# A fast matrix product for two of three channels, with its four PSUM banks in one tile

## The chip, the core and the metric

The kernel runs on one core of one Trainium2 chip. The metric is device time in microseconds, the median of several runs of one execution each. Lower is better. The engines are TensorE (PE, with its weight loads PEld), VectorE (DVE), ScalarE (ACT) and GpSimd (POOL); SyncE (SP) issues most DMAs.

## What is computed

A map x of 384 x 384 positions with 128 channels goes through two layers. Only the first one's middle matters here:

```python
z = layernorm(x)
left  = (z @ Wl + bl) * sigmoid(z @ Wlg + blg)
right = (z @ Wr + br) * sigmoid(z @ Wrg + brg)
core  = einsum('bikh,bjkh->bijh', left, right)      # 128 products of 384 x 384 x 384
zo    = layernorm(core) @ Wout + bout               # normalised over h
x1    = x + sigmoid(x @ Wg + bg) * zo
```

The second layer is a gated row update of x1. The norm over h after the core needs, for every position (i, j), the sum over channels of core and of its square.

## The kernel before

Three stages follow each other. Stage 1 makes left and right for all positions and writes them to DRAM (lr_d). Stage 2 forms the core, one channel h at a time. Stage 3 does the rest, row by row. The change touches stage 2 alone.

**Layout of stage 2.** N is 384, P is 128, NB is 3, J is N/2 = 192. A channel's left and right matrices lie in SBUF as three row blocks of 128 (index k of the product) by 384. `load_h(h)` loads both, interleaved, into `loaded2[h]` by two DMAs on SP's queue; three channels are in flight, and a channel's load is issued when TensorE has finished the channel three before. The last two groups of 64 positions never left SBUF (`kept`), and `stay(h)` copies them in on POOL. `apart(h, k)` (L632) copies block k of right out of the interleaved tile to `right[h]` on ScalarE.

**Two forms of the product.** For even h, `plain` issues nine products of 128 x 128 by 128 x 384 into `pc`, a PSUM tile of three banks, one bank for each row block of the result. For odd h a form after Strassen and Winograd covers the upper 256 rows: `left_sums` (four sums of 128 x 128 on POOL, L618) and `right_sums2` (three instructions on POOL, L623 to L628) form sums of blocks ahead of time, and TensorE then needs eleven half-width products (128 x 192) into `b0` to `b3`, besides three full ones into `b4` for the last 128 rows. In full widths this is 8.5 instead of 9. `b0` to `b4` are five PSUM tiles of one bank each. The order in the odd channel is:

1. the first product into b0; three into b4; ScalarE copies b0 to SBUF (`one`);
2. one product each into b1, b2, b3;
3. four adds on VectorE of 192 columns combine these (`base`, `more2`, `least`; L651);
4. seven more half products into b0, b1, b3, b2, the first of them into b0 again;
5. four more adds of 192 columns write the result's upper rows to SBUF (`ct`).

**Sums and stores.** ScalarE copies `pc` or `b4` to `ct`, squares each finished `ct` into `sq` (part of the SBUF tile `arena`, L635), and VectorE adds `ct` to `csum` (L638) and `sq` to `csq` (L642), 1152 columns at a time. For an even channel the sum is read from `pc`. `store_core` (L645) issues the DMA of `ct` to DRAM.

**What sets the order.** Every instruction passes through `seq`, which keeps each engine's instructions in the order of the text. The engines run side by side. The waits between them are placed by the tile framework from the tiles that each instruction reads and writes; the kernel states none. The last two channels (126 and 127) are written out after the loop and use `plain`'s order. All products of the loop pass through the helper `product` (L648), so that the profile tells them apart by their tiles: `pc` for the plain form, `b` for the other.

In stage 1, which isn't changed, one more PSUM tile of several banks matters for the prediction: `pr`, `[P, 2, 512]`. Two products (L372) fill its two banks; ScalarE reads both (L383), then VectorE (L385).

Of the kernel before, what the change touches and what calls it, by code (L numbers as in the profile page):

```python
# [8 lines left out]
F32 = mybir.dt.float32  # L9
# [5 lines left out]
P = 128  # L15
# [4 lines left out]
def triangle_then_gated_row_kernel(ctx: ExitStack, tc: tile.TileContext, a: dict, out: bass.AP):  # L20
# [35 lines left out]
    def seq(ins):  # L56

        return tc.keep_in_program_order(ins)
# [21 lines left out]
    with ExitStack() as ctx2:  # L80
# [480 lines left out]

        with tc.tile_pool(name="p2r", bufs=2, side="right", reuse_waits="tile") as rrp, \
             tc.tile_pool(name="p2more", bufs=1, side="right", reuse_waits="tile") as more, \
             tc.tile_pool(name="p2out", bufs=3, side="right", reuse_waits="tile") as op, \
             tc.tile_pool(name="p2st", bufs=1, side="right", reuse_waits="tile") as stp:
            csum = spool.tile([P, NB, N], F32, name="csum")
            csq = spool.tile([P, NB, N], F32, name="csq")
            seq(nc.vector.memset(csum, 0.0))
# [26 lines left out]

            J = N // 2
            js = slice(0, J), slice(J, N)
            one, base, more2, least = (arena[:, n, j] for n in (2, 2 * NB) for j in js)
            tt = arena[:, 0:2].rearrange("p b n -> p (b n)").rearrange("p (q j) -> p q j", j=J)
            ss = [arena[:, 2 * NB + 1, n * P:(n + 1) * P] for n in range(3)] + [stp.tile([P, P], F32, name="s4")]  # L600
            sq = arena[:, NB:2 * NB]
            cts = {}

            def block(h, k, i):
                return loaded2[h][:, k, i * P:(i + 1) * P, 0]

            def stay(h):

                for (kb, ig), lrt in kept.items():
                    seq(nc.gpsimd.tensor_copy(loaded2[h][:, kb, ig * G:(ig + 1) * G], lrt[:, h]))  # L610

            def left_sums(h):

                for n, x, y, op in ((0, block(h, 0, 1), block(h, 0, 0), ALU.subtract),
                                    (1, block(h, 0, 1), block(h, 1, 1), ALU.add),
                                    (2, ss[1], block(h, 0, 0), ALU.subtract),
                                    (3, block(h, 1, 0), ss[2], ALU.subtract)):
                    seq(nc.gpsimd.tensor_tensor(ss[n], x, y, op))  # L618

            def right_sums2(h):  # L620

                rr = right[h]
                seq(nc.gpsimd.tensor_tensor(  # L623
                    tt[:, 0:2], rr[:, 0, js[1]].unsqueeze(1).to_broadcast([P, 2, J]),
                    rr.rearrange("p b n -> p (b n)").rearrange("p (a m) -> p a m", a=2)[:, :, js[0]], ALU.subtract,
                ))
                seq(nc.gpsimd.tensor_tensor(tt[:, 2], rr[:, 0, js[0]], tt[:, 1], ALU.subtract))
                seq(nc.gpsimd.tensor_tensor(tt[:, 3], rr[:, 1, js[0]], tt[:, 2], ALU.subtract))  # L628

            def apart(h, k):  # L630

                seq(nc.scalar.copy(right[h][:, k], loaded2[h][:, k, :, 1]))  # L632

            def squares(h):
                seq(nc.scalar.activation(sq, cts[h], AF.Square))  # L635

            def add_sum(h, c=None):
                seq(nc.vector.tensor_add(csum, c or cts[h], csum))  # L638

            def add_squares(h):  # L640
                if h >= 0:
                    seq(nc.vector.tensor_add(csq, csq, sq))  # L642

            def store_core(h, queue=nc.sync):
                seq(queue.dma_start(out=core_d[:, h, :].rearrange("(b p) j -> p b j", p=P), in_=cts[h]))  # L645

            def product(to, lhsT, rhs, start=True, stop=True):
                seq(nc.tensor.matmul(to, lhsT=lhsT, rhs=rhs, start=start, stop=stop))  # L648

            def add(out, ps, term):  # L650
                seq(nc.vector.tensor_add(out, ps, term))  # L651

            def plain(h, banks):

                for k in range(NB):
                    for i in range(NB):
                        product(banks[i], block(h, k, i), right[h][:, k], k == 0, k == NB - 1)

            fill(0)
            with tc.tile_pool(name="p2mix", bufs=1, space=PSUM, reuse_waits="tile") as mps:  # L660
                pc = mps.tile([P, NB, 512], F32, name="pc")
                b0, b1, b2, b3 = (mps.tile([P, 512], F32, name="b%d" % n)[:, :J] for n in range(4))
                b4 = mps.tile([P, 512], F32, name="b4")[:, :N]
                for h in range(H - 2):
                    cts[h] = op.tile([P, NB, N], F32, tag="ct", name="ct")
                    right[h + 1] = rrp.tile([P, NB, N], F32, tag="rr", name="rr")
                    if h % 2 == 0:
                        plain(h, [pc[:, i, :N] for i in range(NB)])
                        if h > 0:
                            store_core(h - 1)  # L670
                        add_squares(h - 2)
                        stay(h + 1)
                        left_sums(h + 1)
                        for k in range(NB - 1):
                            apart(h + 1, k)
                        right_sums2(h + 1)
                        if h > 0:
                            squares(h - 1)
                            add_sum(h - 1)
                        apart(h + 1, NB - 1)  # L680
                        if h > 0:
                            add_squares(h - 1)
                    else:
                        rr, ct = right[h], cts[h]
# [4 lines left out]
                        seq(nc.scalar.copy(cts[h - 1], pc[:, :, :N]))  # L689
                        store_core(h - 1)  # L690
                        add_sum(h - 1, pc[:, :, :N])
                        seq(nc.scalar.copy(one, b0))
                        stay(h + 1)
                        for k in range(NB - 1):
                            apart(h + 1, k)
                        seq(nc.scalar.copy(ct[:, 2], b4))
                        apart(h + 1, NB - 1)
                        squares(h - 1)
                        product(b1, ss[2], tt[:, 2])
                        product(b2, ss[0], tt[:, 1])  # L700
                        product(b3, ss[1], tt[:, 0])
                        add(base, b1, one)
                        add(more2, b2, base)
                        add(base, b3, base)
                        add(least, b2, base)
                        product(b0, block(h, 1, 0), B[1][0], True, False)
                        product(b0, block(h, 2, 0), B[2][0], False, True)
                        product(b1, ss[3], B[1][1], True, False)
                        product(b1, block(h, 2, 0), B[2][1], False, True)
                        product(b3, block(h, 1, 1), tt[:, 3], True, False)  # L710
                        product(b3, block(h, 2, 1), B[2][0], False, True)
                        product(b2, block(h, 2, 1), B[2][1])
                        add(ct[:, 0, js[0]], b0, one)
                        add(ct[:, 0, js[1]], b1, base)
                        add(ct[:, 1, js[0]], b3, more2)
                        add(ct[:, 1, js[1]], b2, least)
                    del right[h], loaded2[h]
                    load_h(h + 3)
                store_core(h)
            with tc.tile_pool(name="p2ps", bufs=2, space=PSUM, reuse_waits="tile") as ps, \  # L720
                 tc.tile_pool(name="p2one", bufs=1, space=PSUM, reuse_waits="tile") as ps1:
                for h in range(H - 2, H):
# [11 lines left out]
                            start=(kb == 0), stop=(kb == NB - 1),  # L734
                        ))
                    if h == H - 2:
                        add_squares(h - 2)
                        squares(h - 1)
                        add_sum(h - 1)
                        add_squares(h - 1)  # L740
# [365 lines left out]
```

## Time and profile before

| | |
|---|---|
| median of 3 runs | 3137.58 us (3137.32 to 3138.57) |
| the profiled execution | 3139.36 us, its span 3137.6 us |
| granted TensorE clock | 0.999 |
| busy: PE, PEld, DVE, ACT, POOL | 99%, 70%, 82%, 62%, 76% of the span |
| stage 2 (the loop) | about 1012 to 1726 us of the span |
| HBM | 253 GB/s over the span |

The span runs from the first instruction to the last of one profiled execution; its own time is given by the device for the same execution and is 1.8 us longer. Matmul ends are modelled, so that a busy TensorE is not one at its peak. A line such as `L651 DVE TENSOR_TENSOR arena<-b,arena 128x192` names the line of the kernel, the engine, the operation, what it writes and reads, and the shape; after the bar come the busy time in us and the mean of one in ns, then the idle time of the engine ahead of the group, and what ended it.

### The profile page before, as it was taken

Reading aid. Unit: us, or ns where it says so; the run is one execution under the profiler, and the core shown is the slowest. Engines: PE = TensorE matmul, PEld = TensorE weight load, DVE = VectorE, ACT = ScalarE, POOL = GpSimd, SP = SyncE. Lnnn points to the kernel's source line nnn. Section 1 sums busy time; section 2 is a strip of 40 time slices with the busy share of each in tenths; the row PEclk is TensorE's granted clock in tenths of the full one; section 3 lists DMA queues with packets and bytes.
Section 4 is the critical chain, followed back from the end, with each engine's and each line's share of the span. In section 5 each row is a group of like instructions: output and inputs, shape, how many; then the busy total and the mean of one; then the engine's idle time right before and its main releaser. Section 6 shows DMA issues by size and latency. Waiting matters only on the chain.

```text
span 3137.6 us, 47186 instructions
## 1 busy us (share of the span) xinstructions
PE 3117.4 (99%) x11936; PEld 2209.1 (70%) x11936; DVE 2581.1 (82%) x7913; ACT 1949.7 (62%) x4196; POOL 2369.4 (76%) x3003
## 2 busy tenths in 40 slices
PE   9999999999999999999999999999999999999998
PEld 4677777777777777777777666777777777777776
DVE  8888888888886777777776888888888888888998
ACT  4444444444444666656666577777777777777776
POOL 6888888888886565666566588787887887888887
PEclk9999999999999999999999999999999999999999
DMA  4888978788883999999999866666666666666562
GB/s 153 327 312 293 334 276 332 287 321 311 292 333 89 288 289 291 291 290 290 290 290 290 296 213 221 217 222 222 222 222 222 220 223 215 222 218 222 205 216 105
DMA packets 509119, 797.61 MB, mean 254 GB/s; under 512 B 56689, under 2 KB 419569, under 8 KB 492466
## 3 DMA queue, kind: packets, MB, share of 16 engines
q1 hardware_dynamic: 507952, 793.20, 74.5%
q8 instruction: 100, 1.64, 0.2%
q14 instruction: 169, 1.38, 0.1%
q10 hardware_dynamic: 834, 1.18, 0.1%
q0 software_dynamic: 64, 0.20, 0.0%
HBM read 508.14 MB, written 286.36 MB: 253 GB/s over the span
## 4 chain that ended last, share of the span: by engine, by line
PE 98%; DVE 1%; ACT 0%; POOL 0%; issue 0%; DMA 0%; SPq 0%; POOLq 0%; DVEq 0%; ACTq 0%
PE pr L372 31%; PE pc L648 12%; PE b L648 11%; PE py L904 8%; PE pr L875 8%; PE pg L892 8%; PE pl L893 8%; PE pg L844 8%; PE py L905 4%; PE pc L732 0%; DMA stage<-in_x_nat_dram 0%; PE pq L852 0%; PE pt L335 0%; POOL rs L286 0%; DVE lr L385 0%
## 5 line engine op out<-in xcount | busy, mean ns | idle before, releaser
L372 PE MATMUL pr<-wz,xc 128*128 128x512 f32 x2176 | 935.2, 592 | 1.4 <-POOL xc L324 1.4
L372 PEld LDWEIGHTS pr<-wz,xc 128*128 128x128 f32 x2176 | 670.5, 308 | 265.4 <-POOL xc L324 2.7
L383 ACT ACTIVATE sg<-pr,rs 128x256 f32<-128x256 f32 x1152 | 482.8, 470 | 510.8 <-ACT sg L383 355.5
L385 DVE SCALAR_TENSOR_TENSOR lr<-pr,rs,sg 128x256 f32<-128x256 f32 x1152 | 501.9, 477 | 165.6 <-ACT sg L383 160.1
L939 ACT ACTIVATE py<-py,nm,rs 128x128 f32<-128x128 f32 x1149 | 491.9, 429 | 158.5 <-DVE u L897 80.0
L904 PEld LDWEIGHTS py<-wo,u 128*128 128x128 f32 x2304 | 376.6, 191 | 97.5
L904 PE MATMUL py<-wo,u 128*128 128x128 f32 x2304 | 402.0, 275 | 0.0
L866 POOL TENSOR_TENSOR cs<-ct,rt 128x384 f32<-128x384 f32 x380 | 378.7, 998 | 9.5 <-PE pr L875 4.1
L974 POOL TENSOR_TENSOR yt<-yt,lnb 128x384 f32<-128x384 f32 x380 | 379.8, 1001 | 2.9 <-DVE yt L968 2.5
L648 PE MATMUL pc<-rr,lrh 128*128 128x384 f32 x1134 | 376.1, 486 | 0.4 <-DVE lr L385 0.4
L324 POOL TENSOR_TENSOR xc<-xc,bc 128x512 f32<-128x512 f32 x272 | 345.6, 1270 | 24.0
L286 POOL TENSOR_TENSOR rs<-nd,mhalf 128x8 f32<-128x8 f32 (+1 forms) x145 | 236.2, 1629 | 147.0 <-ACT sg L383 107.4
L919 DVE BATCH_NORM_STATS2 st<-py 128x6 f32<-128x128 f32 x1152 | 266.1, 286 | 88.6 <-PE py L905 86.7
L905 PE MATMUL py<-ident,x1T 128*128 128x128 f32 x1152 | 314.0, 273 | 0.0
L875 PE MATMUL pr<-cs,wc 128*128 128x384 f32 x768 | 313.5, 490 | 0.0
L892 PE MATMUL pg<-x1T,mat_L_conv_W_gate 128*128 128x384 f32 x768 | 310.7, 486 | 0.9 <-ACT g L895 0.9
L632 ACT COPY rr<-lrh 128x384 f32<-128x384 f32 x378 | 205.0, 553 | 171.5 <-DMA lrh<-lr_d 108.4
L844 PE MATMUL pg<-xt,mat_L_conv_Wg 128*128 128x384 f32 x768 | 310.7, 487 | 0.3 <-ACT ct L758 0.2
L648 PEld LDWEIGHTS pc<-rr,lrh 128*128 128x128 f32 x1134 | 220.3, 196 | 128.4 <-issue 1.1
L893 PE MATMUL pl<-x1T,mat_L_conv_W_left 128*128 128x384 f32 x768 | 310.5, 486 | 0.0
L618 POOL TENSOR_TENSOR arena<-lrh 128x128 f32<-128x128 f32 x126 | 105.4, 837 | 259.4 <-DMA lrh<-lr_d 206.4
L895 ACT ACTIVATE g<-pg,col_L_conv_b_gate 128x384 f32<-128x384 f32 x384 | 222.7, 580 | 104.4 <-PE pg L892 93.9
(151 smaller groups left out, 5278.9 us busy)
## 6 DMA issues: line engine op xcount, KB each, us to landing
lr_d<-lr SPq DMA_DIRECT2D x128, 1024.0 KB
lrh<-lr_d SPq DMA_DIRECT2D x128, 640.0 KB
xt<-in_x_row_dram SPq DMA_DIRECT2D x96, 768.0 KB
ct<-core_d SPq DMA_DIRECT2D x95, 768.0 KB
rt<-rstd_d SPq DMA_DIRECT2D x95, 768.0 KB
core_d<-ct SPq DMA_DIRECT2D x126, 576.0 KB
out_dram<-yt SPq DMA_DIRECT2D x94, 768.0 KB
xt<-in_x_nat_dram SPq DMA_DIRECT2D x136, 512.0 KB
```

Of the source, the lines that this page charges most:

```text
L372: seq(nc.tensor.matmul(pr[:, r, :], lhsT=columns[n][:, 4 * q + i, :] if n < PLAIN else columns[n][:, q, :, i], rhs=wz, start=True, stop=Tr ...
L383: seq(nc.scalar.activation(sg[r], pr[:, r, 2 * H:], AF.Sigmoid, scale=rs[r]))
L385: seq(nc.vector.scalar_tensor_tensor(t[:, :, c * XR + r0 + r, :], pr[:, r, :2 * H].rearrange("k (h s) -> k h s", s=2), rs[r], sg[r].rearra ...
L648: seq(nc.tensor.matmul(to, lhsT=lhsT, rhs=rhs, start=start, stop=stop))
L844: seq(nc.tensor.matmul(pg[:, :N], lhsT=wg0, rhs=r["xT"], start=True, stop=True))
L875: seq(nc.tensor.matmul(pr[:, :N], lhsT=wc, rhs=r["cs"], start=True, stop=True))
L892: seq(nc.tensor.matmul(pg2[:, :N], lhsT=wgate, rhs=r["x1T"], start=True, stop=True))
L893: seq(nc.tensor.matmul(pl[:, :N], lhsT=wleft, rhs=r["x1T"], start=True, stop=True))
L904: seq(nc.tensor.matmul(py[:, s], lhsT=r["u"][:, s], rhs=r["wo"], start=True, stop=False))
L905: seq(nc.tensor.matmul(py[:, s], lhsT=r["x1T"][:, s], rhs=ident, start=False, stop=True, is_transpose=True))
L939: seq(nc.scalar.activation(py[:, s], py[:, s], AF.Identity, bias=bias, scale=scale))
L974: seq(engine.tensor_tensor(yt, yt, lnbb, ALU.add))
```

## The change

The channels of the loop now go by `h % 3`. Kind 0 is plain; kinds 1 and 2 take the form with one half-width product less. There are two sets of the sums of blocks (`sss`, `tts`), one for each of the kinds; the second set's left sums lie in `wz`, a weight tile that stage 1 no longer needs. `b0` to `b3` are now slices of one PSUM tile `bb` of four banks, so that an add can take two banks at once: one add makes two of the middle terms, `join` writes row block 0 of the result from banks 0 and 1, and `close` row block 1 from banks 2 and 3. For kind 1, `join` comes at the channel's end and `close` in the next channel; for kind 2, both come in the next one. `close` is followed by the store and by the sum.

Squares now go to PSUM: those of a kind 0 channel over `pc` itself, those of kind 1 into `pc`, those of kind 2 into `bb` during the plain channel. VectorE then adds them to `csq` from there, for kind 1's squares in three adds, one for each bank. The core of the diff:

```diff
-                b0, b1, b2, b3 = (mps.tile([P, 512], F32, name="b%d" % n)[:, :J] for n in range(4))
+                bb = mps.tile([P, 4, 512], F32, name="bb")
+                b0, b1, b2, b3 = (bb[:, n, :J] for n in range(4))
+                def close(h):
+                    add(cts[h][:, 1].rearrange("p (q j) -> p q j", j=J), bb[:, 2:4, :J], terms2[:, 2:4])
+                def join(h):
+                    add(cts[h][:, 0].rearrange("p (q j) -> p q j", j=J), bb[:, 0:2, :J], terms2[:, 0:2])
                 for h in range(H - 2):
...
-                    if h % 2 == 0:
+                    kind, rr, ct = h % 3, right[h], cts[h]
+                    if kind == 0:
                         plain(...)
                         if h > 0:
+                            join(h - 1)
+                            close(h - 1)
                             store_core(h - 1)
+                            add_sum(cts[h - 1])
-                        add_squares(h - 2)
                         stay(h + 1); left_sums(h + 1); apart(h + 1, 0..1); right_sums2(h + 1)
-                            squares(h - 1)
-                            add_sum(h - 1)
+                            squares(cts[h - 1], bb[:, :NB, :N])
                         apart(h + 1, NB - 1)
-                            add_squares(h - 1)
+                            add_squares(bb[:, :NB, :N])
                     else:
                         product(b0, ...); three products into b4
-                        seq(nc.scalar.copy(cts[h - 1], pc[:, :, :N]))
+                        if kind == 1:
+                            seq(nc.scalar.copy(cts[h - 1], pc))
+                            add_sum(pc)
+                        else:
+                            close(h - 1)
+                            add_sum(cts[h - 1])
                         store_core(h - 1)
-                        add_sum(h - 1, pc[:, :, :N])
-                        seq(nc.scalar.copy(one, b0))
+                        seq(nc.scalar.copy(terms2[:, 0], b0))
                         stay(h + 1)
+                        if kind == 1: left_sums(h + 1)
                         apart(h + 1, 0..1)
+                        if kind == 1: right_sums2(h + 1); squares(pc, pc)
+                        else: squares(cts[h - 1], pc)
                         seq(nc.scalar.copy(ct[:, 2], b4))
                         apart(h + 1, NB - 1)
-                        squares(h - 1)
                         product(b1, ss[2], tt[:, 2])
-                        product(b2, ss[0], tt[:, 1])
-                        product(b3, ss[1], tt[:, 0])
-                        add(base, b1, one)
-                        add(more2, b2, base)
-                        add(base, b3, base)
-                        add(least, b2, base)
+                        product(b2, ss[1], tt[:, 0])
+                        product(b3, ss[0], tt[:, 1])
+                        add(base, b1, terms2[:, 0])
+                        add(terms2[:, 1:3], bb[:, 2:4, :J], base.unsqueeze(1).to_broadcast([P, 2, J]))
+                        add(terms2[:, 3], b3, terms2[:, 1])
                         seven products into b0, b0, b1, b1, then the banks of row block 1
-                        add(ct[:, 0, js[0]], b0, one)
-                        add(ct[:, 0, js[1]], b1, base)
-                        add(ct[:, 1, js[0]], b3, more2)
-                        add(ct[:, 1, js[1]], b2, least)
+                        if kind == 1:
+                            join(h)
+                            add_squares(pc)
+                        else:
+                            for ib in range(NB):
+                                seq(nc.vector.tensor_add(csq[:, ib], pc[:, ib], csq[:, ib]))
                     load_h(h + 3)
+                join(h)
+                close(h)
                 store_core(h)
```

After the loop, channel 126 squares and adds the last loop channel as before, without the add of squares that was left over.

More of the change, by code (lines that the diff above doesn't have):

```diff
@@ L563, in triangle_then_gated_row_kernel @@
              tc.tile_pool(name="p2more", bufs=1, side="right", reuse_waits="tile") as more, \
-             tc.tile_pool(name="p2out", bufs=3, side="right", reuse_waits="tile") as op, \
-             tc.tile_pool(name="p2st", bufs=1, side="right", reuse_waits="tile") as stp:
+             tc.tile_pool(name="p2out", bufs=3, side="right", reuse_waits="tile") as op:
             csum = spool.tile([P, NB, N], F32, name="csum")
@@ L597, in triangle_then_gated_row_kernel @@
             js = slice(0, J), slice(J, N)
-            one, base, more2, least = (arena[:, n, j] for n in (2, 2 * NB) for j in js)
-            tt = arena[:, 0:2].rearrange("p b n -> p (b n)").rearrange("p (q j) -> p q j", j=J)
-            ss = [arena[:, 2 * NB + 1, n * P:(n + 1) * P] for n in range(3)] + [stp.tile([P, P], F32, name="s4")]
+            terms2 = arena[:, 2:4].rearrange("p b n -> p (b n)").rearrange("p (q j) -> p q j", j=J)
+            base = arena[:, 6, js[0]]
+            tts = [arena[:, n:n + 2].rearrange("p b n -> p (b n)").rearrange("p (q j) -> p q j", j=J) for n in (0, 4)]
+            sss = [[arena[:, 2 * NB + 1, n * P:(n + 1) * P] for n in range(3)] + [arena[:, 6, J:J + P]],
+                   [wz[:, n * P:(n + 1) * P] for n in range(4)]]
             sq = arena[:, NB:2 * NB]
@@ L612, in left_sums @@
             def left_sums(h):
+                ss = sss[h % 3 - 1]
                 for n, x, y, op in ((0, block(h, 0, 1), block(h, 0, 0), ALU.subtract),
@@ L620, in right_sums2 @@
             def right_sums2(h):
-                rr = right[h]
+                rr, tt = right[h], tts[h % 3 - 1]
                 seq(nc.gpsimd.tensor_tensor(
@@ L632, in apart, with squares, add_sum, add_squares @@
                 seq(nc.scalar.copy(right[h][:, k], loaded2[h][:, k, :, 1]))
[L634 to L642, printed above, removed]
+            def squares(c, out):
+                seq(nc.scalar.activation(out, c, AF.Square))
+            def add_sum(c):
+                seq(nc.vector.tensor_add(csum, c, csum))
+            def add_squares(c):
+                seq(nc.vector.tensor_add(csq, c, csq))
             def store_core(h, queue=nc.sync):
@@ L660, in triangle_then_gated_row_kernel @@
             with tc.tile_pool(name="p2mix", bufs=1, space=PSUM, reuse_waits="tile") as mps:
-                pc = mps.tile([P, NB, 512], F32, name="pc")
-                b0, b1, b2, b3 = (mps.tile([P, 512], F32, name="b%d" % n)[:, :J] for n in range(4))
+                pc = mps.tile([P, NB, 512], F32, name="pc")[:, :, :N]
+                bb = mps.tile([P, 4, 512], F32, name="bb")
                 b4 = mps.tile([P, 512], F32, name="b4")[:, :N]
+                b0, b1, b2, b3 = (bb[:, n, :J] for n in range(4))
[3 more added lines that the diff above has]
+                    add(cts[h][:, 0].rearrange("p (q j) -> p q j", j=J), bb[:, 0:2, :J], terms2[:, 0:2])
                 for h in range(H - 2):
@@ L666, in triangle_then_gated_row_kernel @@
                     right[h + 1] = rrp.tile([P, NB, N], F32, tag="rr", name="rr")
-                    if h % 2 == 0:
-                        plain(h, [pc[:, i, :N] for i in range(NB)])
+                    kind, rr, ct = h % 3, right[h], cts[h]
+                    if kind == 0:
+                        plain(h, [pc[:, i] for i in range(NB)])
                         if h > 0:
+                            join(h - 1)
+                            close(h - 1)
                             store_core(h - 1)
-                        add_squares(h - 2)
+                            add_sum(cts[h - 1])
                         stay(h + 1)
@@ L677, in triangle_then_gated_row_kernel @@
                         if h > 0:
-                            squares(h - 1)
-                            add_sum(h - 1)
+                            squares(cts[h - 1], bb[:, :NB, :N])
                         apart(h + 1, NB - 1)
                         if h > 0:
-                            add_squares(h - 1)
+                            add_squares(bb[:, :NB, :N])
                     else:
-                        rr, ct = right[h], cts[h]
+                        ss, tt = sss[kind - 1], tts[kind - 1]
                         B = [[rr[:, k, j] for j in js] for k in range(NB)]
@@ L688, in triangle_then_gated_row_kernel @@
                             product(b4, block(h, k, 2), rr[:, k], k == 0, k == NB - 1)
-                        seq(nc.scalar.copy(cts[h - 1], pc[:, :, :N]))
+                        if kind == 1:
[4 more added lines that the diff above has]
+                            add_sum(cts[h - 1])
                         store_core(h - 1)
-                        add_sum(h - 1, pc[:, :, :N])
-                        seq(nc.scalar.copy(one, b0))
+                        seq(nc.scalar.copy(terms2[:, 0], b0))
                         stay(h + 1)
+                        if kind == 1:
+                            left_sums(h + 1)
                         for k in range(NB - 1):
                             apart(h + 1, k)
+                        if kind == 1:
+                            right_sums2(h + 1)
+                            squares(pc, pc)
+                        else:
+                            squares(cts[h - 1], pc)
                         seq(nc.scalar.copy(ct[:, 2], b4))
                         apart(h + 1, NB - 1)
-                        squares(h - 1)
                         product(b1, ss[2], tt[:, 2])
-                        product(b2, ss[0], tt[:, 1])
-                        product(b3, ss[1], tt[:, 0])
-                        add(base, b1, one)
-                        add(more2, b2, base)
-                        add(base, b3, base)
-                        add(least, b2, base)
+                        product(b2, ss[1], tt[:, 0])
[3 more added lines that the diff above has]
+                        add(terms2[:, 3], b3, terms2[:, 1])
                         product(b0, block(h, 1, 0), B[1][0], True, False)
@@ L709, in triangle_then_gated_row_kernel @@
                         product(b1, block(h, 2, 0), B[2][1], False, True)
-                        product(b3, block(h, 1, 1), tt[:, 3], True, False)
-                        product(b3, block(h, 2, 1), B[2][0], False, True)
-                        product(b2, block(h, 2, 1), B[2][1])
-                        add(ct[:, 0, js[0]], b0, one)
-                        add(ct[:, 0, js[1]], b1, base)
-                        add(ct[:, 1, js[0]], b3, more2)
-                        add(ct[:, 1, js[1]], b2, least)
+                        product(b2, block(h, 1, 1), tt[:, 3], True, False)
+                        product(b2, block(h, 2, 1), B[2][0], False, True)
+                        product(b3, block(h, 2, 1), B[2][1])
+                        if kind == 1:
+                            join(h)
+                            add_squares(pc)
+                        else:
+                            for ib in range(NB):
+                                seq(nc.vector.tensor_add(csq[:, ib], pc[:, ib], csq[:, ib]))
                     del right[h], loaded2[h]
                     load_h(h + 3)
+                join(h)
+                close(h)
                 store_core(h)
@@ L736, in triangle_then_gated_row_kernel @@
                     if h == H - 2:
[L737 to L740, printed above, removed]
+                        squares(cts[h - 1], sq)
+                        add_sum(cts[h - 1])
+                        add_squares(sq)
                         fill(h + 1)
```

## The prediction

> **What bounds the kernel now.** I read the page's chain of waits first. It is TensorE nearly everywhere:
>
> ```profile
> PE 98%; DVE 1%; ACT 0%; POOL 0%; issue 0%; DMA 0%; SPq 0%; POOLq 0%; DVEq 0%; ACTq 0%
> ```
>
> The change lies in the stage of the core products (L648), so next the busy time by stretch, cut to that stage. The columns are stretch, length, then PE, PEld, DVE, ACT, POOL, granted clock, DMA share, GB/s.
>
> ```profile
> 1300.00:1400.00 100.00, 100.00 (x409) 73.24 (x408) 71.27 (x108) 59.67 (x97) 60.01 (x97) 1.00 0.98 291
> ```
>
> TensorE is never idle here; no other engine reaches three quarters. DMA at 0.98 looks full, but bytes per channel stay the same, so only a faster TensorE could press on it. Third, the chain in order of time (start, length, what):
>
> ```profile
> 1046.83 5.80 PE pc L648 x18
> 1052.63 5.51 PE b L648 x28
> 1058.14 5.80 PE pc L648 x18
> ```
>
> A plain channel takes 5.80 us, one with a half-width product less 5.51. A full product is 5.80/9 = 0.644, a half one (5.51 - 3 x 0.644)/11 = 0.325. Nothing lies between channels. The 126 channels of the loop take 63 x 11.31 = 712.5 us. The stage's waits show 0.4 us of TensorE waiting for POOL in 500 us: nothing to win there.
>
> Fourth, the groups by form in 1100:1600 give durations (after the bar: busy us, mean ns):
>
> ```profile
> L651 DVE TENSOR_TENSOR arena<-b,arena 128x192 f32<-128x192 f32 x180 | 64.4, 358 | 17.9 <-PE b L648 0.5
> L638 DVE TENSOR_TENSOR csum<-pc,csum 128x1152 f32<-128x1152 f32 x45 | 61.1, 1357 | 81.4 <-ACT ct L689 81.4
> L638 DVE TENSOR_TENSOR csum<-ct,csum 128x1152 f32<-128x1152 f32 x44 | 62.4, 1417 | 0.0
> L635 ACT ACTIVATE arena<-ct 128x1152 f32<-128x1152 f32 x89 | 103.7, 1165 | 0.0
> L692 ACT COPY arena<-b 128x192 f32<-128x192 f32 x44 | 14.3, 325 | 0.0
> ```
>
> Between 192 and 1152 columns an add grows by (1357 - 358)/960 = 1.04 ns a column, so the new 384-wide adds are estimated at 0.56 us.
>
> Fifth, what a wait costs, from two timelines (start, us, engine):
>
> ```profile
> 1312.72 2.42 PE L648 MATMUL b<-rr,lrh 128*128 128x192 f32 x8
> 1312.92 1.12 ACT L689 COPY ct<-pc 128x1152 f32<-128x1152 f32 x1 [2.29 <-PE pc L648]
> 1315.57 1.67 DVE L651 TENSOR_TENSOR arena<-b,arena 128x192 f32<-128x192 f32 x4
> ...
> 1042.66 0.59 POOL L627 TENSOR_TENSOR arena<-rr,arena 128x192 f32<-128x192 f32 x1
> 1043.31 0.95 PEld L648 LDWEIGHTS b<-arena 128*128 128x128 f32 x6 [0.61 <-POOL arena L627]
> ```
>
> A reader starts 0.20 us after TensorE turned to its next product (1312.72 to 1312.92). Four adds of 0.358 in 1.67 leave 0.24: about 0.10 between an add and one that needs its result. TensorE resumes 0.06 us after its releaser ends (1043.25 to 1043.31).
>
> **The view that decides.** b0 to b3 are four tiles of one PSUM bank each. The change makes them one tile, bb, of four banks. Does a wait then go by bank or by tile? Stage 1 has such a tile: pr, two banks, a product into each, each read by ScalarE, then by VectorE. Its timeline where nothing else runs:
>
> ```profile
> 994.67 17.33 PE L372 MATMUL pr<-wz,xc 128*128 128x512 f32 x40
> ...
> 998.35 0.84 ACT L383 ACTIVATE sg<-pr,rs 128x256 f32<-128x256 f32 x2 [0.88 <-ACT sg L383]
> 999.22 0.88 DVE L385 SCALAR_TENSOR_TENSOR lr<-pr,rs,sg 128x256 f32<-128x256 f32 x2 [0.84 <-ACT sg L383]
> ```
>
> The banks are filled 0.87 us apart (two records each, 17.33/20). Yet ScalarE's two reads run together: two of 0.47 in 0.84. The first sat until the second bank was done. VectorE starts at 999.22, when both reads of ScalarE have ended (998.35 + 0.84), though its first operand was ready at 998.82. So the framework that places the waits orders the users of a PSUM tile as a whole, reads included. (In SBUF it looks at the region: TensorE reads parts of the tile arena while POOL writes others.)
>
> **What the skill says.** PSUM — Partial Sum Buffer, section PSUM bank collisions: two engines must not touch the same bank and partition quadrant at once; different banks may be used in parallel. The hardware thus doesn't ask for the waits above, and the trace shows them nevertheless. GPSIMD Engine Reference, Specifications: POOL contends with VectorE instructions with two SBUF inputs. The trace agrees: POOL's L618 takes from 0.46 us up to 1.69 beside csum<-ct and csq<-arena, while L627 stays at 0.59 beside csum<-pc. TensorE: Matmul & The Clock Gate, What's actually happening: the clock falls after an idle window of about 3.4 us; no run here shows that, and I use it for a rival alone.
>
> **The change, part by part.**
>
> Products: the Strassen-like form goes from 63 to 84 of the loop's channels. 21 x (5.80 - 5.51) = **6.1 us less**, all on the path.
>
> Load on the others, per three channels (16.82 us of products). VectorE: kind 0 0.56 + 0.56 + 1.42 + 1.36; kind 1 1.36 + 0.36 + 0.56 + 0.36 + 0.56 + 1.36; kind 2 0.56 + 1.42 + 0.36 + 0.56 + 0.36 + 3 x 0.56: 13.4 us. ScalarE: nine copies of rr at 0.55, three squares at 1.17, one copy of pc 1.12, two of b0 0.33, two of b4 0.48: 11.2. POOL: two sets of sums of 5.95 (3.43 for the four L618, then 1.33, 0.59, 0.60) and six L610 at 0.29: 13.7, less where two-SBUF adds leave. All fit; each costs nothing as long as no order forces it onto the path. Squares into PSUM I take at 1.17 like before (ScalarE: Activation LUTs, Step-by-step, calls writes to PSUM faster: at most less). The removed tile s4 and the second set of sums in wz change addresses only. Stores: those of Strassen channels now wait for close, some 0.5 us later. On SP the two loads behind a store wait for TensorE to end the channel anyhow, and the landing of a store is awaited by nobody near: 0.
>
> The waits on bb. Time 0 is a channel's first product. b0 and b4 end at 2.26, the first b1, b2, b3 at 3.24. If users of bb are ordered as a whole:
>
> - VectorE reads b1 only after b3: 3.24 + 0.20 = 3.44. base 0.36, gap 0.10, the two-block add 0.56, gap 0.10, terms2[3] 0.36: 4.92.
> - TensorE's next b0 needs all of bb released: 4.92 + 0.06 = 4.98. It was free at 3.24: **1.74 us idle, in each of 84 channels**. In the kernel before, b0's second product needed only the old copy of b0, and b1's only the first add.
> - The last seven halves end 2.28 later, at 7.26.
> - Kind 1 only: join then runs 7.46 to 8.02, and kind 2's first product, also in bb, starts at 8.08: **0.82 idle, 42 times**. Behind it on VectorE: add_squares(pc) to 1.25 of kind 2, close to 1.81, add_sum to about 3.3: just free for base at 3.44. ScalarE's copy of b0 must follow close (1.87 to 2.20), so b1 starts at 2.26, on time: 0, at most 0.1.
> - Kind 2 to 0: the three csq adds end at about 6.5, before plain's pc at 7.25; join and close have plain's 5.80 us as cover: 0. Were that cover gone, they'd cost 1.1.
> - Kind 0 to 1: close at 1.3, squares after the second rr copy (2.7 in the trace before, earlier with loads less pressed) to 3.9, add_squares to 5.3, before 5.80: 0, at most 0.1.
>
> Sum: 84 x 1.74 + 42 x 0.82 = 146 + 34 = 180 us more, 6 less: +174. Unseen costs: the two-block add reads two banks and a broadcast term, which no row shows; 0.50 to 0.70 each, I take 0.56 (-5 to +12 over 84). A reader's start may be 0.1 off either way at 126 turns (-13 to +13), the restart at best immediate (126 x 0.06: -8), the two turns that I set to 0 at most 0.1 each (+8). Together -26 to +33.
>
> Against its own time: the profiled execution took 3139.4 (span 3137.6), 1.8 over the median 3137.6. 3139.4 + 174 - 1.8 = **3311 us**.
>
> **Rivals.**
>
> *Waits by bank* (not slower). Place: bb within a Strassen channel. Then base starts after b1, b2's second product needs the two-block add at about 4.2 and has its slot at 4.54; join ends at 5.2 with b0 due at 5.51; csq of bank 0 ends at 5.2 with pc due at 5.51. All are covered by 0.3 to 0.5, and the 6.1 us are kept but for late loads ahead of squares in kind 0, estimated at 0 to 0.1 us each time (up to 4 us): 3131.5 to 3136, say 3132.5. For: the hardware asks for no more, and SBUF tiles are treated by region. Against: stage 1. It decides from 6.1/42 = 0.15 us of waits per three channels: below that no loss.
>
> *By tile, and the clock falls too.* TensorE would be idle for a fifth of the stage. If each gap of 1.74 dropped the granted clock to half for one 3.4 us window (half of that, 1.7, is lost): 84 x 1.7 = 143 more, 3454. Against: the gaps are half of that window, and the page shows 0.9 or more in every slice.
>
> *VectorE becomes the bound.* 13.4 of 16.82 us is 80%: only if each wait lasted longer than it now does. With waits by bank and 0.3 us lost at each of two turns, 42 x 0.6 = 25 - 6: 3157. For: small slacks; against: TensorE's waits in the trace before (0.4 us in 500).
>
> That fewer products are issued can't fail: it is counted in the program.
>
> **How the numbers follow.** By tile: 0.90, at 3311. By bank: 0.07. Clock: 0.02. VectorE: 0.01. The likeliest case with its bounds is 3285 to 3344; that holds about 0.9 of its 0.90, so it is my range. 0.2% (6.3 us) is about what a measurement of this kernel can tell from no change. By bank the gain is at most 6.1 plus the few tenths of old waits, so 0.03 of its 0.07 goes to faster and 0.04 to same; slower 0.93.
>
> **What would show it.** In the stage, waits of PE for DVE arena (the add into terms2[3]) near 146 us in 84 pieces of 1.7, and for DVE ct (join) near 34 in 42; TensorE near 80% there; a Strassen channel of 7.3 or 8.1 us, plain still 5.80; clock 1.00; POOL's L618 nearer 0.5. I'm wrong if base starts before b3's product ends, or if the second b0 follows the first b3 at once.

## Result and the profile after

| | before | after |
|---|---|---|
| median | 3137.86 us (4 runs) | 3320.66 us (4 runs, 3319.67 to 3322.08) |
| ratio, 95% interval | 1 | 1.0583 [1.0564, 1.0601] |
| span of the profiled execution | 3137.6 us | 3320.3 us |
| granted TensorE clock | 0.999 | 0.998 |

The changed kernel is 182.8 us slower. The prediction, 3311 us, was 9.7 us low and its range held the time.

The page's chain of waits: TensorE gives up 5 points of it, to VectorE and to "issue".

```profile
PE 93%; DVE 4%; issue 2%; ACT 1%; POOL 0%; DMA 0%; DVEq 0%; POOLq 0%; ACTq 0%
```

The same stretch of the stage as was shown for before (stretch, length, then busy us of PE, PEld, DVE, ACT, POOL, clock, DMA share, GB/s):

```profile
1300.00:1400.00 100.00, 82.99 (x351) 61.27 (x351) 61.13 (x86) 45.23 (x78) 49.17 (x89) 1.00 0.76 229
```

TensorE was busy for all of these 100 us and is now idle for 17 of them, at full clock. No other engine is busier than before: VectorE fell from 71 to 61, DMA from 0.98 to 0.76. So no engine has become the bound; the engines wait for each other. What TensorE waits for is in the view of waits, 1100:1700 (who waits, for whom; us in all, times, longest). This stretch has 56 Strassen-like channels:

```profile
ACT arena L707 <- DVE ct L652: 143.5, 28, 5.1
DVE ct L652 <- PE bb L649: 109.0, 56, 2.6
PEld bb L649 <- DVE arena L652: 100.7, 56, 1.8
...
PE bb L649 <- DVE arena L652: 84.2, 56, 1.5
```

There are 56 waits for an add into arena, one in each of these channels (PEld is the weight load and PE the product of the same wait). ScalarE's copy of b0 (L707) behind close has a longer line, but TensorE isn't delayed by it: the products behind the copy, the x6 of a channel, take 0.99 us in kind 2 as in kind 1. The chain in order of time (start, length, what) shows where the wait stands, in a plain channel and the kind 1 channel after it:

```profile
1310.18 5.80 PE pc L649 x18
1315.98 0.33 PE bb L649 x2
1316.31 1.94 PE b L649 x6
1318.24 0.99 PE bb L649 x6
...
1319.33 0.37 DVE arena L652
...
1319.72 0.57 DVE arena L652
...
1320.31 0.37 DVE arena L652
...
1320.72 2.55 PE bb L649 x14
1323.28 0.70 issue
1323.97 0.57 PE bb L649 x2
```

The profile counts two records for each product. After the first products into b1, b2 and b3 (the x6) TensorE stands still for all three adds, base among them, and only then starts the seven last half products (x14). The 0.70 of "issue" is the second wait: the timeline has join inside it, from 1323.31 for 0.56 us, and TensorE's next product 0.10 us after its end:

```profile
1320.72 0.93 PE L649 MATMUL bb<-rr,lrh 128*128 128x192 f32 x4 [1.51 <-DVE arena L652]
...
1322.46 0.81 PE L649 MATMUL bb<-rr,lrh 128*128 128x192 f32 x4
1323.31 0.56 DVE L652 TENSOR_TENSOR ct<-bb,arena 128x384 f32<-128x384 f32 x1 [2.65 <-PE bb L649]
...
1323.97 0.41 PE L649 MATMUL bb<-rr,lrh 128*128 128x192 f32 x1 [0.70 <-issue]
```

The profile names no releaser here. TensorE's weight loads held a semaphore wait until 1323.92, 0.05 us after join's end. A copy on POOL (L611) ends at the same time, but TensorE doesn't wait for it: in two_pairs below these copies run until 1317.78 at the same turn, and TensorE goes on at 1317.19.

From the start of one kind 2 channel (1302.64) to that of the next (1323.97) are 21.33 us for three channels. Before, three of them took 1.5 x 11.31 = 16.97. Over 42 such groups that is 42 x 4.36 = 183 us, the whole difference.

### The profile page after: what moved, and what is told of

It is laid out like the page before. It is cut to its first block, busy times and chain, and to the rows that moved or that the text cites. A ratio compares the mean times of both kernels' runs of the same rounds, so it can differ in the third digit from the quotient of the medians.

```text
span 3320.3 us, 47399 instructions
## 1 busy us (share of the span) xinstructions
PE 3146.2 (95%) x12146; PEld 2234.1 (67%) x12146; DVE 2610.5 (79%) x7913; ACT 1935.8 (58%) x4217; POOL 2395.5 (72%) x3150
## 4 chain that ended last, share of the span: by engine, by line
PE 93%; DVE 4%; issue 2%; ACT 1%; POOL 0%; DMA 0%; DVEq 0%; POOLq 0%; ACTq 0%
PE pr L372 29%; PE bb L649 10%; PE py L927 8%; PE pr L898 8%; PE pg L915 7%; PE pl L916 7%; PE pc L649 7%; PE pg L867 7%; PE b L649 5%; PE py L928 4%; DVE arena L652 3%; PE pt L335 0%; PE pc L756 0%; PE pq L875 0%; POOL rs L286 0%
## 5 line engine op out<-in xcount | busy, mean ns | idle before, releaser
L649 PE MATMUL bb<-rr,lrh 128*128 128x192 f32 x1008 | 232.7, 340 | 155.9 <-DVE arena L652 126.7
L649 PEld LDWEIGHTS bb<-rr,lrh 128*128 128x128 f32 x1008 | 171.5, 197 | 202.3 <-DVE arena L652 151.5
L869 ACT ACTIVATE gT<-pg,col_L_conv_bg 128x384 f32<-128x384 f32 x384 | 220.9, 578 | 102.5 <-PE pg L867 102.5
L947 POOL TENSOR_TENSOR rs<-rs,mhalf 128x6 f32<-128x6 f32 x192 | 256.5, 1336 | 16.0
```

## Experiments

My theory: the framework places a wait on a PSUM tile as a whole, so that four banks in one tile make TensorE wait for reads of banks it doesn't touch. The main rival: the waits come from something else in the change, such as the order of the adds, the squares or the copies. Two kernels tell them apart: one has only the merged tile, the other all but the merged tile. A second suspect is the argument reuse_waits="tile" of stage 2's pools. No run is without it, but the traces speak against it: pr's pool in stage 1 doesn't have it and shows the wait, while arena's pool has it and arena goes by region (in before TensorE loads from arena at 1303.34 while POOL writes another part of it until 1303.56).

**1. merge_only.** The kernel before with `bb` and nothing else of the change.

```diff
-                b0, b1, b2, b3 = (mps.tile([P, 512], F32, name="b%d" % n)[:, :J] for n in range(4))
+                bb = mps.tile([P, 4, 512], F32, name="bb")
+                b0, b1, b2, b3 = (bb[:, n, :J] for n in range(4))
```

> The kernel before, with nothing changed but that b0 to b3 are slices of one four-bank PSUM tile. Theory (waits go by PSUM tile): in each of the 63 odd channels TensorE's second product into b0 waits for the four adds. They start 0.20 us after b3's first product and take 0.36 + 0.10 + 0.36 + 0.10 + 0.36 + 0.04 + 0.36 = 1.68; with the restart as the changed kernel shows it (its chain of 1.48 cost 1.78) that is 1.98 us each: 63 x 1.98 = 125, so about 3263 us (3250 to 3275). Rival (waits go by bank; the loss of the changed kernel comes from the new order of VectorE's work or from the two-bank adds): 3138, no change.

Measured: 3261.0 us (3260.64 to 3262.0), ratio 1.0394 [1.0378, 1.041]. Its waits in 1100:1600 and one channel of its chain:

```profile
PEld bb L648 <- DVE arena L651: 75.6, 38, 2.0
PE bb L648 <- DVE arena L651: 64.4, 38, 1.7
```

```profile
1310.42 0.99 PE bb L648 x6
...
1313.10 2.55 PE bb L648 x14
1315.65 5.80 PE pc L648 x18
```

The same wait, now behind four adds. No instruction of this kernel differs from the kernel before in what it computes or in its place in the text; only the four banks are now one tile, and that costs 123 us, 1.96 in each of 63 channels. The theory holds; the rival can't explain this run.

**2. two_pairs.** The changed kernel with `bb` cut into `lo` (b0, b1) and `hi` (b2, b3), so that the adds of two banks stay. Kind 0's squares and their add, which spanned three banks, go in two instructions each.

```diff
-                bb = mps.tile([P, 4, 512], F32, name="bb")
-                b0, b1, b2, b3 = (bb[:, n, :J] for n in range(4))
+                lo, hi = (mps.tile([P, 2, 512], F32, name=n) for n in ("lo", "hi"))
+                b0, b1, b2, b3 = (t[:, n, :J] for t in (lo, hi) for n in range(2))
```

> The changed kernel with bb cut into two tiles of two banks, lo (b0, b1) and hi (b2, b3); the two-at-a-time adds stay, squares and their add in kind 0 become two instructions each. Theory by tile: the 1.7 us waits go, as base reads lo alone. What is left: in kind 2 base comes at 3.1 behind add_sum and b0's second product at 3.24 waits for it, about 0.4; the plain channel's first product waits for all three csq adds of pc, still one tile, about 0.35; hi at most 0.1. 42 x 0.85 = 36, less 6 for the products: 3168 us (3150 to 3190). Rival (VectorE's work itself, whatever the tiles): the same instructions, so near 3320.

Measured: 3153.26 us (3152.86 to 3155.39), ratio 1.0051 [1.0038, 1.0065]: 167 of the 183 us are gone. What is left of the waits (1100:1600), and where the chain of a kind 2 channel has the second (b0's second product is the first of the x8, which takes 1.30 without a wait):

```profile
PEld pc L649 <- issue: 8.4, 28, 0.4
PEld lo L649 <- DVE arena L652: 5.5, 29, 0.2
```

```profile
1303.06 1.48 PE lo L649 x8
1304.54 0.97 PE hi L649 x6
```

Both are again read as waits for a tile: b0's second product waits for base's read of b1, and the plain channel waits for the last read of any bank of `pc` (the next run cuts `pc`, and this wait goes).

**3. mended.** two_pairs with `pc` cut into one bank and two banks, each copied, summed and squared by itself, and with two sums on VectorE moved to where it has time.

```diff
-                pc = mps.tile([P, NB, 512], F32, name="pc")[:, :, :N]
+                p0 = mps.tile([P, 512], F32, name="p0")[:, :N]
+                p12 = mps.tile([P, 2, 512], F32, name="p12")[:, :, :N]
```

> As two_pairs, and pc is cut into a tile of one bank and one of two, and the sums of finished channels are moved: kind 1's from kind 2 to kind 0 behind join and close, kind 2's to the end of kind 0, so that base in kind 2 isn't late. Theory by tile: no wait of TensorE is left, or a few hundredths: 3137.9 - 6.1 - 0.5 (old waits for POOL) = 3131 us, up to 3137 if one of the turns costs 0.1 us each time. Rival: near 3320, or over 3200 if VectorE's load sets the pace.

Measured: 3138.45 us (3136.07 to 3140.9), ratio 1.0004 [0.9996, 1.0012]. The wait ahead of the plain channel is gone, but the time stops at that of before, above the 3131 to 3137 us that were expected. The chain:

```profile
1310.19 1.38 PE lo L649 x8
1311.57 0.98 PE hi L649 x6
```

The x8 still takes 0.08 us too long. 84 x 0.08 = 6.7 us, about the 6.1 that the fewer products should gain. The timeline has base and, behind it, the weight load of b0's second product:

```profile
1309.22 0.68 PEld L649 LDWEIGHTS hi<-arena 128*128 128x128 f32 x4
...
1309.58 0.36 DVE L652 TENSOR_TENSOR arena<-lo,arena 128x192 f32<-128x192 f32 x1 [0.79 <-PE lo L649]
1309.99 0.64 PEld L649 LDWEIGHTS lo<-rr,lrh 128*128 128x128 f32 x4
```

The four loads ahead of it start 0.16 us apart, so it was due at 1309.87; it started at 1309.99, just after base's end at 1309.94.

**4. mended2.** b1's first product goes ahead of b4's last, so that it ends 0.65 us earlier against b0's second product, and ScalarE copies b0 behind its first copy of rr.

```diff
                         for k in range(NB):
+                            if k == NB - 1:
+                                product(b1, ss[2], tt[:, 2])
                             product(b4, block(h, k, 2), rr[:, k], k == 0, k == NB - 1)
...
                         product(b3, ss[0], tt[:, 1])
-                        product(b1, ss[2], tt[:, 2])
```

> As mended, where a channel of the new form took 5.59 us instead of 5.51: the weight load of b0's second product, due some 0.16 us ahead of its product, waited for base. Here b1's first product goes ahead of the last product into b4, so that base can start 0.65 us earlier; the copy of b0 moves behind the first rr copy on ScalarE. If the 0.08 us come from that wait, they go: 84 x 0.08 = 6.7 less than mended, about 3131.5 us (3130 to 3134). If they are a fixed cost of the form with tiles of two banks, or if ScalarE's copy of b0 now comes too late, 3138 or more.

Measured: 3137.4 us (3136.03 to 3139.07), ratio 1.0001 [0.9993, 1.0009]. A miss, and the chain shows why: the 0.08 us only moved from the x8 to the x6, to b2's second product.

```profile
1308.60 1.30 PE lo L649 x8
1309.90 1.06 PE hi L649 x6
```

base no longer decided (1307.69 to 1308.05, where b0's second product starts at 1308.43; it came 0.29 us earlier and not 0.65, since it now waited for the copy of b0). The two-block add starts when b2 and b3 are both complete, and the add into terms2[3] behind it ends at 1309.59:

```profile
1308.63 0.95 DVE L652 TENSOR_TENSOR arena<-hi,arena 128x384 f32<-128x384 f32 x2 [0.59 <-PE hi L649]
...
1309.70 0.31 PEld L649 LDWEIGHTS hi<-arena,lrh 128*128 128x128 f32 x2
```

That is 0.02 us after the weight load of b2's second product was due (1309.57); the load started at 1309.70.

**5. mended4.** The first products of b2 and b3 too go ahead of b4's last product, and ScalarE copies b0 at once.

```diff
                             if k == NB - 1:
                                 product(b1, ss[2], tt[:, 2])
+                                product(b2, ss[1], tt[:, 0])
+                                product(b3, ss[0], tt[:, 1])
```

> mended2 with the first products of b2 and b3 moved, behind b1's, ahead of the last product into b4, and with ScalarE's copy of b0 issued right behind b0's first product. In mended2 the Strassen channel still took 5.59 us: the 0.08 us had moved from b0's second product to b2's (hi x6 took 1.06 us, 0.98 due), because the two-block add starts only when b2 and b3 are complete and the add into terms2[3] behind it reads the tile hi until 0.13 us after the next weight load for it is due. With two b4 passes (0.65 us) between b3's first product and that weight load, VectorE's chain has slack. Theory (each leftover 0.08 us is a tile's late release): Strassen channels 5.51 us, 84 x 0.08 = 6.7 us off mended2, 3131 us (3129.5 to 3133). Rival (the 0.08 us is a fixed price of a weight load that has several semaphores to look at, wherever it stands): channels stay at 5.59 us and the time at 3137 us.

Measured: 3157.46 us (3156.77 to 3158.73), ratio 1.0064 [1.0052, 1.0077], far from both forecasts. This kernel doesn't compute the core: in kind 2, close reads b2 and b3 only after the new channel's products have been written to them, so that row block 1 of every kind 1 channel is wrong. Its waits can be read all the same. The last products of hi are on time now (x6 in 0.97), but the chain has new steps in kind 2:

```profile
1303.28 0.56 DVE ct L652
1303.83 0.27 DVE arena L652
1304.11 0.04 issue
1304.15 1.57 PE lo L649 x8
```

close (the `ct` line) stood ahead of base on VectorE and waited for the new b2 and b3. A product moved ahead in the text had been moved past close as well, and base was late by all of close. The x6 at 0.97 already speaks against a fixed price of that weight load; the total says nothing on it.

**6. mended5.** mended4 with close ahead of kind 2's products, and in kind 1 the copies of the plain channel ahead of the copy of b0.

```diff
+                        if kind == 2:
+                            close(h - 1)
                         product(b0, block(h, 0, 0), B[0][0])
```

> mended4 with two orders put right that its trace shows late: in kind 2 VectorE's close of the channel before is issued ahead of the channel's own products (in mended4 b2's first product went ahead of it, so that close stood behind the new b2 and b3 and base behind close), and in kind 1 ScalarE copies the plain channel's sum before it copies b0 (in mended4 VectorE's add_sum, and base behind it, waited for those copies). By mended2's times, in kind 2 close ends 0.6 us before b2's product is due, and in kind 1 add_sum ends 0.1 us before b1's first product does. Theory (late releases of a tile only): no waits, Strassen channels 5.51 us, 84 x 0.08 = 6.7 us off mended2: 3131 us (3129.5 to 3133). Rival (fixed price of the weight load): 5.59 us and 3137 us.

Measured: 3134.29 us (3131.73 to 3139.66), ratio 0.9995 [0.9987, 1.0004]; the profiled execution, 3131.73, is the fastest. A kind 1 channel of its chain, and the start of the kind 2 channel after it:

```profile
1302.59 0.33 PE lo L649 x2
1302.92 1.29 PE b L649 x4
1304.21 0.33 PE lo L649 x2
1304.53 0.65 PE hi L649 x4
1305.18 0.65 PE b L649 x2
1305.83 1.30 PE lo L649 x8
1307.13 0.97 PE hi L649 x6
1308.10 0.33 PE lo L649 x2
```

1308.10 - 1302.59 = 5.51: no wait at all. So the leftover 0.08 us was a late release and no fixed price of the weight load. In 29 of 41 groups of three channels the trace has 16.82 or 16.83 us, the sum of the products, and the loop takes 709.5 us where before took 713.7: 4.2 of the 6.1 us. The rest of this execution's lead lies outside the loop. The median is 3 us above the forecast and outside its range, and the runs spread over 8 us. The weight loads' waits in the whole stage:

```profile
PEld lo L649 <- POOL arena L629: 6.1, 20, 0.9
PEld p L649 <- DVE csq L643: 2.7, 5, 0.8
PEld lo L649 <- issue: 2.7, 16, 0.2
```

b1's product, now earlier, sometimes meets POOL's sum tt[2] (L629) not yet ready. Of the stage's 84 such sums 41 took 1.58 to 1.76 us, each beside VectorE's add of `ct` to `csum`; the other 43 ran beside none and took 0.59 or 0.60. In before all 63 took 0.59 or 0.60. Since mended both of these adds stand in the plain channel, where POOL makes the sums for kind 1. That this makes the spread between runs is likely, but not shown.

**7. pr_split, pr_split_timed.** The sign by which I chose the theory was stage 1's two-bank tile `pr`. Here the kernel before gets two one-bank tiles in its place; the tiles p0 and p1, which share its buffers, become one-bank tiles too.

```diff
-                pr = pps.tile([P, 2, 4 * H], F32, tag="pr", name="pr")
+                pr = [pps.tile([P, 4 * H], F32, tag="pr%d" % r, name="pr%d" % r) for r in range(2)]
```

> The kernel before, with stage 1's two-bank tile pr as two tiles of one bank. Theory by tile: ScalarE's two reads no longer run back to back but some 0.87 us apart, each right behind its own product, and VectorE's first read starts after ScalarE's first, not its second; the time stays within 0.2%, since TensorE sets the pace there. Rival (the pairing comes from elsewhere, the banks or ScalarE's own order): pairs as before, 0.84 us for two.

> pr_split again, timed. If stage 1's start and end really gain by the finer waits: 3134.5 us (3133 to 3136). If its single time was chance: 3137.6.

Measured: 3136.66 us in a single run, then 3135.09 us (3134.7 to 3136.49), ratio 0.9994 [0.9986, 1.0002]. The timeline of stage 1 (the two readers' lines):

```profile
998.80 0.47 ACT L383 ACTIVATE sg<-pr,rs 128x256 f32<-128x256 f32 x1 [0.39 <-PE pr L372]
...
999.30 0.48 DVE L385 SCALAR_TENSOR_TENSOR lr<-pr,rs,sg 128x256 f32<-128x256 f32 x1 [0.37 <-ACT sg L383]
```

ScalarE's reads, which came in pairs behind both products, now come singly, each behind its own product, and VectorE starts 0.03 us after its one operand instead of behind ScalarE's second read. The sign meant what I took it for. In time the median gains some 2 us, and the interval doesn't exclude nothing; TensorE was already the bound there.

**8. Both together.** mended2_pr and mended5_pr add the edit of 7 to 4 and 6.

> mended2 and pr_split together: stage 1's pr in two tiles of one bank. In pr_split stage 2 began at 1008.9 us of the span instead of 1012.4. If that holds, some 3 us below mended2: about 3128.5 us (3127 to 3132). If the start differed by chance, the same as mended2.

> mended4 with stage 1's pr as two one-bank tiles. Theory: the two gains add, 3131 - 2 = 3129 us (3127 to 3131). Rival (fixed price of the weight load): 3135 us, as in mended2_pr.

> mended5 with stage 1's pr as two one-bank tiles. Theory: the two gains add, 3131 - 2 = 3129 us (3127 to 3131). Rival (fixed price of the weight load): 3135 us, as in mended2_pr.

Measured: mended2_pr 3135.09 us (3134.57 to 3137.17), ratio 0.9994 [0.9986, 1.0003]; mended4_pr 3156.76 us (3155.88 to 3160.27), 1.0061 [1.0047, 1.0075]; mended5_pr 3133.29 us (3131.44 to 3137.43), 0.999 [0.9981, 0.9998]. All three lie above the theory's forecasts, and mended4_pr has mended4's fault. The last is the only version whose interval lies below 1, by 0.1%. It is too small to rest a choice on, but it is the change's idea without its loss.

## Why the prediction was right

**The view that decided.** The forecast rested on pr in stage 1 as evidence that waits go by tile. merge_only and two_pairs show this in both directions, pr_split shows it at pr itself. The rival of waits by bank is refuted: base didn't start before b3's product ended.

**The Strassen wait, forecast 1.74, measured 1.79** (7.30 for a kind 1 channel up to join, less 5.51). Three terms were off and nearly cancelled. With time 0 at the first product's start (1315.82), base started at 3.51 instead of 3.44: the 0.20 us that the forecast took was a start of ScalarE, and VectorE's in the same trace of before is 0.27 (TensorE turns from b1 at 1315.30, the first add starts at 1315.57). The three adds took 1.34 in all instead of 1.48, since the gap between dependent adds is 0.03 and not 0.10: of the three gaps in that trace of before, the two of 0.10 have one more semaphore instruction of VectorE in them, the third has none and is 0.03. TensorE resumed at 4.90 instead of 4.98, but its first four passes took 0.93 us where four take 0.81 in the same timeline further on; I hadn't priced that. The view of waits counts 1.50 of the 1.79 (84.2/56), not the 1.7 that I had announced: the product ahead of the wait runs 0.16 beyond its slot (a record lasts 0.33 us, and one starts every 0.16), and the slow restart makes 0.12.

**The join turn, forecast 0.82, measured 0.94**: 0.70 of idle time and 0.24 by which the first two passes (0.57) exceed the usual 0.33. The profile calls this wait "issue", not a wait for DVE ct as I had said it would.

**The sum.** Per three channels (2 x 0.05) + 0.12 = 0.22 us were missing; 42 x 0.22 = 9 us is about the distance between 3311 and 3320.7. It is a difference of larger errors: the restart of TensorE came out 15 us too cheap (84 x 0.12 and, behind join, 42 x 0.12), base's start 6 us too early (84 x 0.07), the adds' gaps 12 us too dear (84 x 0.14). For restarts the forecast had no bound upward at all. The mechanism was right; that the number came within 10 us is in part luck.

**The two-block add and the squares.** The row that was missing before:

```profile
L652 DVE TENSOR_TENSOR arena<-bb,arena 128x384 f32<-128x384 f32 x56 | 31.2, 557 | 1.9
```

0.557 against the estimate of 0.56, broadcast term and all. Squares into PSUM took 1.11 to 1.14 us on average against 1.165 into SBUF: slightly less, as the section of the Trainium skill that I cited (ScalarE: Activation LUTs, Step-by-step) lets one expect.

**What I set to 0** stayed 0 where it was tied to the idle TensorE: the copy of b0 in kind 2 ended at 1304.62, 0.11 us ahead of the next weight load, and the products behind it weren't delayed; plain channels took 5.80; the clock stayed at 1.00; POOL's L620 (L618 before) fell to 0.46 to 0.52 on average. two_pairs shows what some of those zeros owed to the waits: with the long waits gone, 0.3 us at the plain channel and 0.2 at b0 in kind 2 (0.08 in kind 1) came out from behind them. The 3132.5 us of the rival of waits by bank were reached by no median here; mended5, with the tiles cut and the orders changed, came to 3134.3.

**A product less is worth its 6.1 us** only if nothing is late: mended and mended2 saved every one of these products and none of the time, mainly because 0.08 us stood in each Strassen-like channel.

## What to carry to other kernels

Before you put PSUM banks into one tile so that an instruction can take two of them, list who reads and who writes each bank within a period: in these runs users of one bank waited for users of all the others. Cut tiles by what is released together, not by what lies side by side. And when a wait of under 0.1 us is left on a saturated TensorE, ask when the next weight load is due, not the next product: the release has to come before that.

## What the runs showed of the hardware

- A TensorE that resumed from a wait didn't do so at full pace. The weight load waited with the product (both start at 1320.72, where in the steady flow of this trace a load precedes its product by 0.16 us), and the first four passes took 0.93 us instead of 0.81. At join's turn the first pass took 0.41 us instead of 0.33.
- TensorE can lose time to a release that comes before the product's own slot: in mended base had ended at 1309.94 and the product started at 1310.03, yet its weight load, due at 1309.87, was late and pushed all that followed by 0.08 us.
- POOL's sum tt[2] takes 0.59 us, or 1.58 to 1.76 where VectorE adds `ct` to `csum` at the same time, both operands in SBUF (41 of 84 in mended5, 11 of 84 after the change, none of 63 before). POOL's first sum of right (L625) took over 2 us in 30 of 84 channels after the change and in 18 of 63 before, so that its mean rose from 1.32 to 1.44 us; I had expected POOL's sums to become faster.
